# Layer 0 of a two-layer attention kernel rewritten: scores laid out keys by queries, both softmax sums taken by pattern matmuls, weight pairs premultiplied

## The chip, the cores and the metric

The kernel runs on one core of one Trainium2 chip. The metric is the device time of one execution in microseconds (us); for the kernel before it is 9794.67 us, the median of three runs between 9791.2 and 9801.31. The profile is of one further execution of the same program. Its engines are PE (TensorE, the matrix engine, with its weight loads listed apart as PEld), DVE (VectorE), ACT (ScalarE), POOL (GpSimd) and SP (SyncE, which issues transfers).

## The reference

The input `x` has 8 batches of 1024 tokens (64 by 16) of 128 channels, all in fp32. Two layers follow one another.

```python
# layer 0: H = 8 heads, tokens (l, f) and (m, g), 64 by 16
scores = einsum('bhlfc,bhmgc->bhlfmg', q, k) / sqrt(c)
a = softmax(scores, axis=4)          # over m
a = softmax(a, axis=5)               # of the result, over g
z = einsum('bhlfmg,bhmgc->bhlfc', a, v)
z1 = layer_norm(z @ wo.T + bo + x)
x = layer_norm(relu(z1 @ w1.T + b1) @ w2.T + b2 + z1)
# layer 1: additive attention, then a recurrence over the 1024 tokens
Wi = norm(t) @ W.T
scores = einsum('d,bijd->bij', v, tanh(Wi[:, None] + Wi[:, :, None]))
t = t + softmax(scores) @ norm(t)
wx = batch_norm(norm(t) @ W2.T)
y_t = sigmoid(wx_t + y_{t-1} @ V.T);  t = t + y
```

So layer 0 takes two softmaxes in a row over the same 1024 keys of each query: the first sums over the 64 values of m for each g, the second over the 16 values of g for each m. Layer 1 takes a tanh for every pair of tokens; the scores are symmetric, so about half of them are computed.

## The kernel before, in words

All matmuls are fp32. A matmul of the program shows in the trace as two MATMUL instructions over the same columns; a transpose shows as one.

`layer0(b)` is a generator for one batch; each `yield` ends a piece. It transposes `x` into `xT` (channels by tokens). For each of 8 heads it projects `qT`, `kT` (L174, L175) and `vh` (L181, L184). Then for each tile of 128 queries: scores `sc` in PSUM, queries on the partitions and the 1024 keys along the free side (L194); maximum over m (L199), subtraction (L200), exponential on ACT (L203), sum over m (L205), reciprocal (L206), product (L207), second exponential (L209), sum over g (L211), reciprocal (L212) and a product on POOL (L213). Eight transposes on PE and two copies on DVE turn the result into `aT` (L155, L156). For every second query tile, `pz` = `vh` times `aT` (L222), and `po` projects that with `wo` (L228) and is added to `xa` (L233). A query tile is one piece; with 64 tiles, the two layer norms and the feed-forward part, a batch has 71 pieces.

`layer1_attention(b)` goes through eight row blocks of 128 tokens, `it`, of width w = 1024, 896, ..., 128 columns. For each row an ACT tanh fills a `th` buffer (L305; five buffers), and matmuls with a 32-column weight pattern add v times that into 32 partitions of `sa` (L308); the row's group c = 0..3 selects which 32. Columns beyond 512 need a second matmul. After each block come the softmax of the block and its product with B (L316 to L340).

The order. The main loop first runs all of `layer0(0)`. Then, for each batch b, it takes three pieces of `layer1_attention(b)` (each piece is four rows, that is four tanhs) and one of `layer0(b+1)`, until both are done. So 71 layer-0 pieces fall beside the first 213 of 258 attention pieces. The tile framework then decides each engine's final order at compile time: it simulates the program, and gives an engine the oldest instruction in program order that is ready and has a buffer. On the chip each engine's order is fixed. The chip's 8 PSUM banks are shared out as `sc` 2, `sa` 2 and a ring `bank` of 4 for all else.

After the last batch comes the recurrence (L385 to L428), and at its end a branch that would redo it step by step if a bound on V did not hold.

Of the kernel before, what the change touches and what calls it, by code (L numbers as in the profile page):

```python
# [17 lines left out]


@with_exitstack  # L20
def kernel(
    ctx: ExitStack,
    tc: tile.TileContext,
    x: bass.AP,
# [23 lines left out]
):  # L48

    nc = tc.nc
    NB, N, C = x.shape
    H = wq.shape[1]
# [13 lines left out]
        t = keep.tile([P, NT, C], F32, tag=f"xa{b}", name=f"xa{b}")  # L70
        xa.append(t)

    NCH = 64
    LCH = N // NCH
    wx = keep.tile([P, LCH, NCH, NB], F32, tag="wx", name="wx")
    wx_stats = keep.tile([P, NB, N // 512, 6], F32, tag="wx_stats", name="wx_stats")

    def load_x(b):
# [56 lines left out]
    def norm(dst, src, mv, rs, j):  # L135
        nc.vector.tensor_scalar(dst, src, mv[:, j, 0:1], rs[:, j : j + 1], ALU.subtract, ALU.mult)
# [11 lines left out]
    def bank(name):  # L148
        return ps_m.tile([P, 512], F32, tag="bank", name=name)
# [119 lines left out]
    def layer1_attention(b):  # L269
        X = xa[b]  # L270

        def normed_and_projected(w, use):

            B = l1.tile([P, NT, C], F32, tag="B", name="B")
            mv, rs = norm_stats(X, NT, "n1")
            for j in range(NT):
                norm(B[:, j, :], X[:, j, :], mv, rs, j)
            for s in range(NT // 4):
                bT = l1.tile([P, 512], F32, tag="bT", name="bT")
                transposed(bT, [B[:, 4 * s + i, :] for i in range(4)])  # L280
                pw = bank("pw")
                nc.tensor.matmul(pw, w, bT, start=True, stop=True)
                use(s, pw)
            return B

        wiT = l1.tile([P, N], F32, tag="wiT", name="wiT")

        def keep_wi(s, pw):
            nc.vector.tensor_copy(wiT[:, s * 512 : (s + 1) * 512], pw)

        B = normed_and_projected(wa_sb, keep_wi)
        yield


        low = l1.tile([P, NT * (NT - 1) // 2, P], F32, tag="low", name="low")
        for it in range(NT):
            i0 = it * P
            w = N - i0
            sa = ps_a.tile([P, N], F32, tag="sa", name="sa")
            for r in range(32):  # L300

                for c in range(4):
                    i = i0 + 32 * c + r
                    th = l1.tile([P, N], F32, tag="th", name="th", bufs=5)
                    nc.scalar.activation(th[:, :w], wiT[:, i0:], AF.Tanh, bias=wiT[:, i : i + 1])  # L305
                    for s0 in range(0, w, 512):
                        s1 = min(s0 + 512, w)
                        nc.tensor.matmul(  # L308
                            sa[32 * c : 32 * c + 32, s0:s1], vpat[:, 31 - r : 63 - r], th[:, s0:s1],
                            start=(r == 0), stop=(r == 31),  # L310
                        )
                yield
            row = it * (it - 1) // 2
            mine = low[:, row : row + it, :]
            R = l1.tile([P, N], F32, tag="R", name="R")
            nc.vector.tensor_copy(R[:, i0:], sa[:, :w])  # L316
            for j0 in range(it + 1, NT, 4):
                js = range(j0, min(j0 + 4, NT))
                pt = bank("plow")
                for k, j in enumerate(js):  # L320
                    nc.tensor.transpose(pt[:, k * P : (k + 1) * P], R[:, j * P : (j + 1) * P], ident)
                for k, j in enumerate(js):
                    nc.vector.tensor_copy(low[:, j * (j - 1) // 2 + it, :], pt[:, k * P : (k + 1) * P])
            if it:
                nc.vector.tensor_copy(R[:, :i0].rearrange("p (t c) -> p t c", c=P), mine)
            mx = l1.tile([P, 1], F32, tag="mx1", name="mx1", bufs=2)
            nc.vector.tensor_reduce(mx, R, AX.X, ALU.max, negate=True)
            den = l1.tile([P, 1], F32, tag="den", name="den", bufs=2)
            nc.scalar.activation(R, R, AF.Exp, bias=mx, accum_out=den)
            nc.vector.reciprocal(den, den)  # L330
            rT = l1.tile([P, NT, P], F32, tag="rT", name="rT")
            for s in range(NT // 4):
                transposed(
                    rT[:, 4 * s : 4 * s + 4, :],
                    [R[:, (4 * s + i) * P : (4 * s + i + 1) * P] for i in range(4)],
                )
            pc = bank("pc")
            for j in range(NT):
                nc.tensor.matmul(pc[:, :C], rT[:, j, :], B[:, j, :], start=(j == 0), stop=(j == NT - 1))
            nc.vector.scalar_tensor_tensor(X[:, it, :], pc[:, :C], den, X[:, it, :], ALU.mult, ALU.add)  # L340

        def keep_wx(s, pw):
            nc.vector.bn_stats(out=wx_stats[:, b, s, :], in_=pw)
            cs = slice(s * 512 // LCH, (s + 1) * 512 // LCH)
            nc.vector.tensor_copy(
                wx[:, :, cs, b].rearrange("p l c -> p c l"), pw.rearrange("p (c l) -> p c l", l=LCH)
            )

        normed_and_projected(wf_sb, keep_wx)
        yield  # L350
# [17 lines left out]
    main.close()  # L368


    rn = ctx.enter_context(tc.tile_pool(name="rn", bufs=1))
    mv = rn.tile([P, 2], F32, tag="mvb", name="mvb")
    nc.vector.bn_aggr(out=mv, in_=wx_stats.rearrange("p b s k -> p (b s k)"))
# [7 lines left out]


    ys = rn.tile([P, NB, N], F32, tag="ys", name="ys")
    for l in range(LCH):
        nc.vector.tensor_scalar(wx[:, l], wx[:, l], sc, off, ALU.mult, ALU.add)  # L385

    def recurrence_by_chunks(ps_w):  # L390
        HC = NCH // 2
        prev = [None, None]
        for k in range(2 * LCH):
            l = k % LCH
            early = k < LCH
            for half in range(2):
# [11 lines left out]

                    nc.vector.memset(y[:, 0:1, :], 0.0)
                if not early:  # L410
                    steps = ys.rearrange("p b (c l) -> p c b l", l=LCH)
                    nc.vector.tensor_copy(steps[:, c0:c1, :, l], y)
                prev[half] = y

    def output(ps_t, pool):
        n = 0
        for g in range(NT // 4):
            for b in range(NB):
                pt = ps_t.tile([P, 4, C], F32, tag="yt", name="yt")
                for i in range(4):  # L420
                    nc.tensor.transpose(pt[:, i, :], ys[:, b, (4 * g + i) * P : (4 * g + i + 1) * P], ident)
                ot = pool.tile([P, 4, C], F32, tag="ot", name="ot")
                nc.vector.tensor_tensor(ot, pt, xa[b][:, 4 * g : 4 * g + 4, :], ALU.add)
                eng = nc.sync if n % 2 else nc.scalar
                eng.dma_start(
                    out=out[b, 4 * g * P : 4 * (g + 1) * P, :].rearrange("(t p) c -> p t c", p=P), in_=ot
                )
                n += 1  # L428

    with tc.tile_pool(name="ps_w", bufs=2, space=PSUM) as ps_w, tc.tile_pool(  # L430
        name="ps_t", bufs=2, space=PSUM
    ) as ps_t, tc.tile_pool(name="ot", bufs=3) as pool:

        pn = ps_t.tile([P, 4, C], F32, tag="yt", name="pn")
        nc.tensor.matmul(pn[:, 0, :], vf_sb, vf_sb, start=True, stop=True)
        rows = rn.tile([P, 1], F32, tag="rows", name="rows")
        nc.vector.tensor_reduce(rows, pn[:, 0, :], AX.X, ALU.add, apply_absolute_value=True)
        nc.tensor.transpose(pn[0:1, 1, :], rows, ident)
        most = rn.tile([1, 1], F32, tag="most", name="most")
        nc.vector.tensor_reduce(most, pn[0:1, 1, :], AX.X, ALU.max)  # L440
        fits = rn.tile([1, 1], mybir.dt.int32, tag="fits", name="fits")
        nc.vector.tensor_scalar(fits, most, 1.05, None, ALU.is_le)

        recurrence_by_chunks(ps_w)
        output(ps_t, pool)
        fit = nc.values_load(fits[0:1, 0:1], min_val=0, max_val=1,
                             skip_runtime_bounds_check_because="the result of a comparison")


    with tc.If(fit == 0):  # L450
        with tc.tile_pool(name="ps_w1", bufs=2, space=PSUM) as ps_w, tc.tile_pool(
            name="ps_t1", bufs=2, space=PSUM
        ) as ps_t, tc.tile_pool(name="ot1", bufs=3) as pool:
            for t in range(N):
                c, l = t // LCH, t % LCH
                acc = ps_w.tile([P, NB], F32, tag="acc1", name="acc1")
                nc.tensor.matmul(acc, ident, wx[:, l, c, :], start=True, stop=t == 0)
                if t:
                    nc.tensor.matmul(acc, vf_sb, ys[:, :, t - 1], start=False, stop=True)
                nc.scalar.activation(ys[:, :, t], acc, AF.Sigmoid)  # L460
            output(ps_t, pool)


# [55 lines left out]
```

## Time and profile before

| what | value |
|---|---|
| median of three runs | 9794.67 us |
| the profiled execution's own time | 9793.98 us |
| its span, first to last instruction | 9792.2 us |
| PE busy / weight loads busy | 8684.9 us / 3812.2 us |
| ACT busy | 6697.6 us |
| DVE busy | 5528.9 us |
| POOL busy | 1124.6 us |
| first tanh of batch 0, of batch 7 | at 848 us, at 8984 us |
| one batch between (first tanh to first tanh) | 1160 to 1165 us, seven times |

Busy time is the union of an engine's instructions. Matmuls are pipelined and their ends are modelled, so a PE that is busy is not PE at its peak. A wait is idle time of an engine in front of an instruction, named by what ended it last.

### The profile page before, as it was taken

Reading aid. Unit: us, or ns where it says so; the run is one execution under the profiler, and the core shown is the slowest. Engines: PE = TensorE matmul, PEld = TensorE weight load, DVE = VectorE, ACT = ScalarE, POOL = GpSimd, SP = SyncE. Lnnn points to the kernel's source line nnn. Section 1 sums busy time; section 2 is a strip of 40 time slices with the busy share of each in tenths; the row PEclk is TensorE's granted clock in tenths of the full one; section 3 lists DMA queues with packets and bytes.
Section 4 is the critical chain, followed back from the end, with each engine's and each line's share of the span. In section 5 each row is a group of like instructions: output and inputs, shape, how many; then the busy total and the mean of one; then the engine's idle time right before and its main releaser. Section 6 shows DMA issues by size and latency. Waiting matters only on the chain.

```text
span 9792.2 us, 105080 instructions
## 1 busy us (share of the span) xinstructions
PE 8684.9 (89%) x40543; PEld 3812.2 (39%) x40543; DVE 5528.9 (56%) x7379; ACT 6697.6 (68%) x9410; POOL 1124.6 (11%) x551
## 2 busy tenths in 40 slices
PE   6667999889998999989998899988999899998998
PEld 3333344433444334343344334443344433434334
DVE  7775557635675456744577455764567545673002
ACT  1114777766776777767777677776777677777996
POOL 1111111101111011100111011110111101110000
PEclk7778999999999999999999999999999999999999
DMA  1000000000000000000000000000000000000000
GB/s 33 0 0 0 1 1 1 1 1 1 1 1 1 1 1 1 1 1 1 1 1 1 1 1 1 1 1 1 1 1 1 1 1 1 1 1 1 1 1 18
DMA packets 20442, 18.91 MB, mean 2 GB/s; under 512 B 1504, under 2 KB 19040, under 8 KB 19936
## 3 DMA queue, kind: packets, MB, share of 16 engines
q1 hardware_dynamic: 14272, 8.59, 0.3%
q8 instruction: 321, 5.26, 0.2%
q10 hardware_dynamic: 5664, 3.55, 0.1%
q14 instruction: 185, 1.52, 0.1%
HBM read 7.94 MB, written 4.19 MB: 1 GB/s over the span
## 4 chain that ended last, share of the span: by engine, by line
PE 66%; DVE 19%; POOL 7%; ACT 5%; issue 2%; POOLq 0%; DMA 0%; ACTq 0%; DVEq 0%
PE sa L308 35%; PE pz L222 9%; PE sc L194 8%; POOL e L213 6%; PE pt L155 6%; ACT th L305 3%; DVE s L205 3%; DVE s L211 3%; DVE mx L199 3%; DVE e L200 2%; PE pp L174 2%; DVE e L207 2%; DVE aT L156 2%; DVE s L212 1%; PE pv L181 1%
## 5 line engine op out<-in xcount | busy, mean ns | idle before, releaser
L305 ACT ACTIVATE th<-wiT 128x1024 f32<-128x1024 f32 (+7 forms) x8192 | 5631.0, 761 | 1752.2 <-PE sa L308 1497.9
L308 PE MATMUL sa<-th,vpat 128*32 128x512 f32 (+3 forms) x24576 | 5049.2, 500 | 156.9 <-ACT th L305 129.5
L308 PEld LDWEIGHTS sa<-th,vpat 128*32 128x32 f32 x24576 | 1430.5, 109 | 3280.5 <-issue 1691.6
L213 POOL TENSOR_TENSOR e<-e,s 128x1024 f32<-128x1024 f32 x512 | 1071.2, 2092 | 7072.5 <-DVE s L212 3982.1
L194 PE MATMUL sc<-kT,qT 128*128 128x512 f32 x2048 | 1168.4, 669 | 233.8 <-DVE e L200 232.2
L205 DVE TENSOR_REDUCE s<-e 128x16 f32<-128x1024 f32 x512 | 970.4, 1895 | 392.3 <-ACT e L203 389.7
L155 PE MATMUL pt<-ident,e 128*128 128x128 f32 x4096 | 615.2, 298 | 516.5 <-POOL e L213 515.0
L156 DVE COPY aT<-pt 128x512 f32<-128x512 f32 x1024 | 662.8, 685 | 711.1 <-PE pt L155 708.1
L222 PE MATMUL pz<-aT,vh 128*128 128x256 f32 x4096 | 1048.4, 399 | 3.7 <-DVE aT L156 3.7
L209 ACT ACTIVATE e<-e 128x1024 f32<-128x1024 f32 x512 | 538.8, 1052 | 691.2 <-DVE e L207 686.0
L199 DVE TENSOR_REDUCE mx<-sc 128x16 f32<-128x1024 f32 x512 | 623.1, 1217 | 592.6 <-PE sc L194 592.6
L222 PEld LDWEIGHTS pz<-aT,vh 128*128 128x128 f32 x4096 | 756.6, 195 | 380.4 <-issue 182.9
L203 ACT ACTIVATE e<-e 128x1024 f32<-128x1024 f32 x512 | 535.3, 1046 | 489.2 <-DVE e L200 486.1
L155 PEld LDWEIGHTS pt<-ident,e 128*128 128x128 f32 x4096 | 492.4, 152 | 881.3 <-POOL e L213 835.3
L211 DVE TENSOR_REDUCE s<-e 128x64 f32<-128x1024 f32 x512 | 620.6, 1212 | 158.9 <-ACT e L209 156.4
L207 DVE TENSOR_TENSOR e<-e,s 128x1024 f32<-128x1024 f32 x512 | 660.2, 1290 | 6.3
L194 PEld LDWEIGHTS sc<-kT,qT 128*128 128x128 f32 x2048 | 344.0, 200 | 782.4 <-issue 635.2
L200 DVE TENSOR_TENSOR e<-sc,mx 128x1024 f32<-128x1024 f32 x512 | 620.5, 1212 | 10.6 <-DVE mx L199 0.5
L316 DVE COPY R<-sa 128x1024 f32<-128x1024 f32 (+3 forms) x64 | 47.0, 734 | 922.8 <-PE sa L308 922.8
L224 DVE COPY zT<-pz 128x256 f32<-128x256 f32 x256 | 107.8, 421 | 813.8 <-PE pz L222 813.0
L212 DVE RECIPROCAL s<-s 128x64 f32<-128x64 f32 x512 | 277.8, 542 | 6.5
L132 POOL TENSOR_TENSOR n_rs<-n_rs,neg_half 128x8 f32<-128x8 f32 x32 | 52.2, 1638 | 1502.8 <-DVE n_rs L131 1502.8
(92 smaller groups left out, 3286.2 us busy)
## 6 DMA issues: line engine op xcount, KB each, us to landing
xa<-in_x_dram SPq DMA_DIRECT2D x8, 512.0 KB, 7.1
out_dram<-ot ACTq DMA_DIRECT2D x8, 256.0 KB, 2.2
out_dram<-ot SPq DMA_DIRECT2D x8, 256.0 KB, 2.3
wk_sb<-in_wk_dram ACTq DMA_DIRECT2D x1, 512.0 KB, 4.7
wq_sb<-in_wq_dram SPq DMA_DIRECT2D x1, 512.0 KB, 6.4
bv_sb<-in_bv_dram ACTq DMA_DIRECT2D x1, 512.0 KB, 8.3
wv_sb<-in_wv_dram SPq DMA_DIRECT2D x1, 512.0 KB, 8.2
wo_sb<-in_wo_dram SPq DMA_DIRECT2D x1, 512.0 KB, 5.2
```

What stands on the lines that cost most here:

```text
L155: nc.tensor.transpose(pt[:, i * P : (i + 1) * P], t, ident)
L156: nc.vector.tensor_copy(dst, pt[:, : len(tiles) * P])
L194: nc.tensor.matmul(sc[:, cols], qT[:, q0 : q0 + P], kT[:, cols], start=True, stop=True)
L199: nc.vector.tensor_reduce(mx, sc.rearrange("p (m g) -> p g m", g=G), AX.X, ALU.max)
L200: nc.vector.tensor_tensor(e3, sc3, mx.unsqueeze(1).to_broadcast([P, M, G]), ALU.subtract)
L205: nc.vector.tensor_reduce(s1, e.rearrange("p (m g) -> p g m", g=G), AX.X, ALU.add)
L207: nc.vector.tensor_tensor(e3, e3, s1.unsqueeze(1).to_broadcast([P, M, G]), ALU.mult)
L211: nc.vector.tensor_reduce(s2, e3, AX.X, ALU.add)
L213: nc.gpsimd.tensor_tensor(e3, e3, s2.unsqueeze(2).to_broadcast([P, M, G]), ALU.mult)
L222: nc.tensor.matmul(pz[:, :QG], vh[:, t, :], aT[:, t, :], start=(t == 0), stop=(t == NT - 1))
L305: nc.scalar.activation(th[:, :w], wiT[:, i0:], AF.Tanh, bias=wiT[:, i : i + 1])
L308: nc.tensor.matmul(sa[32 * c : 32 * c + 32, s0:s1], vpat[:, 31 - r : 63 - r], th[:, s0:s1], start=(r == 0), stop=(r == 31),)
```

## The change

- Weights are combined once at the start: `A` = Wq'Wk and `Wvo` = Wv'Wo for each head. Scores become `xT`' (A `xT`): one projection `u` in place of q and k. The product with V gives the projected output at once, and the product with `wo` is gone.
- Scores lie keys by queries: 128 keys on the partitions, 512 queries along the free side. A unit of work is one head for 512 queries; 16 units make a batch. The exponentials `e` are then already laid out for the product with V, so the transposes and their copies are gone. No maximum is subtracted; a check computes bounds on the scores.
- Sums over m or over g are now across partitions. They are taken by matmuls with 0/1 patterns of 32 columns: `over_m` (s1) and `over_g` (s2). The reciprocals are spread back by matmuls with `back_m` (r1b) and `back_g` (r2b), and DVE multiplies from PSUM. POOL is out of the loop.
- `x` comes in transposed as well, laid out by the host; `xa` is now written only after the heads.
- The pieces are smaller (four, two or four per phase of a unit) and are handed out in proportion to an estimate of the attention's work, `done`, over the whole attention.
- `sa` keeps 2 banks, `sc` keeps 2 (now two key tiles of 512 queries), `zT` has 1 of its own, and the ring `bank` has 3. The tiles `R`, `rT` and `bT` of layer 1 share the five `th` buffers.
- `check_bounds` reads `x` once more, tile by tile, and forms a flag `fits`. After the fast path a branch runs the old computation, `general_path`, if the flag is 0.

The core of the diff; the removed lines are those of `layer0` and of the main loop printed above.

```diff
+    fast_path(tc, a, fits)
+    fit = tc.nc.values_load(fits[0:1, 0:1], min_val=0, max_val=1, ...)
+    with tc.If(fit == 0):
+        general_path(tc, *[a[n] for n in names.split()])
...
+        for i in range(2):
+            nc.vector.tensor_reduce(over_m[:, i, :], ident.rearrange("p (m g) -> p g m", g=G), AX.X, ALU.add)
...
+        for dst, left, right in ((A, wqn, wkn), (Wvo, wvn, wo)):
+            for g in range(H // 4):
+                pp = bank("pp")
+                for i in range(4):
+                    h = 4 * g + i
+                    nc.tensor.matmul(pp[:, i * C : (i + 1) * C], left[:, h, :], right[:, h, :], start=True, stop=True)
+                nc.vector.tensor_copy(dst[:, 4 * g : 4 * g + 4, :], pp.rearrange("p (h c) -> p h c", c=C))
...
+    def check_bounds():
+        for b in range(NB):
+            two = l0.tile([P, 2, N], F32, tag="e", name="two", bufs=2)
+            xb, sq = two[:, 0, :].rearrange("p (t c) -> p t c", c=C), two[:, 1, :]
+            nc.sync.dma_start(out=xb, in_=a["x"][b].rearrange("(t p) c -> p t c", p=P))
+            nc.gpsimd.tensor_tensor(sq3, xb, xb, ALU.mult)
+            nc.vector.tensor_reduce(n2, sq3, AX.X, ALU.add)
...
+    def layer0(b, xT):
+        for hg in range(2):
+            vp = l0.tile([P, NT, H // 2, C], F32, tag="vp", name="vp")
+            for t in range(NT):
+                pv = bank("pv")
+                nc.tensor.matmul(pv3, xT[:, t * P : (t + 1) * P], Wvo[:, 4 * hg : 4 * hg + 4, :], start=True, stop=True)
+                nc.vector.tensor_copy(vp[:, t], pv3)
+                if t % 2:
+                    yield
+            for qh in range(N // QH):
+                yield from heads(xT, vp, zs, hg, qh)
+        yield from after_heads(X, zs)
+
+    def heads(xT, vp, zs, hg, qh):
+        zT = ps_z.tile([P, QH], F32, tag="zT", name="zT")
+        for h in range(4 * hg, 4 * hg + 4):
+            pu = bank("pu")
+            nc.tensor.matmul(pu, A[:, h, :], xT[:, q0 : q0 + QH], start=True, stop=True)
+            nc.vector.tensor_scalar(u, pu, ub[:, h : h + 1], None, ALU.add)
+            e = l0.tile([P, NT, QH], F32, tag="e", name="e", bufs=2)
+            s1 = bank("s1")
+            for tp in range(NT // 2):
+                sc = ps_s.tile([P, 2, QH], F32, tag="sc", name="sc")
+                for i in range(2):
+                    nc.tensor.matmul(sc[:, i, :], xT[:, t * P : (t + 1) * P], u, start=True, stop=True)
+                nc.scalar.activation(e[:, 2 * tp : 2 * tp + 2, :], sc, AF.Exp, scale=SCALE)
+                for i in range(2):
+                    for qc in range(4):
+                        nc.tensor.matmul(
+                            s1[32 * qc : 32 * qc + 32, :P], over_m.rearrange("p i g -> p (i g)"),
+                            e[:, t, qc * P : (qc + 1) * P], start=t == 0, stop=t == NT - 1,
+                        )
+                yield
+            nc.vector.reciprocal(r1, s1[:, :P])
+            r1b = bank("r1b")
+            for qc in range(4):
+                nc.tensor.matmul(r1b[:, qc * P : (qc + 1) * P], back_m[:, qc].rearrange("p m g -> p (m g)"), r1, ...)
+            s2 = bank("s2")
+            for tq in range(2):
+                nc.vector.tensor_tensor(e4, e4, r1b.unsqueeze(1).to_broadcast([P, 4, QH]), ALU.mult)
+                nc.scalar.activation(e4, e4, AF.Exp)
+                for i in range(4):
+                    for q in range(2):
+                        r0 = 32 * (2 * q + tq)
+                        nc.tensor.matmul(
+                            s2[r0 : r0 + 32, :256], over_g[:, i].rearrange("p i m -> p (i m)"),
+                            e[:, 4 * tq + i, q * 256 : (q + 1) * 256], start=i == 0, stop=i == 3,
+                        )
+                yield
+            nc.vector.reciprocal(r2, s2[:, :256])
+            for t in range(NT):
+                r2b = bank("r2b")
+                for q in range(2):
+                    nc.tensor.matmul(r2b[:, q * 256 : (q + 1) * 256], back_g[:, t, q].rearrange("p m g -> p (m g)"), r2, ...)
+                nc.vector.tensor_tensor(e[:, t, :], e[:, t, :], r2b, ALU.mult)
+                nc.tensor.matmul(zT, vp[:, t, h % 4, :], e[:, t, :], ...)
+                if t % 2:
+                    yield
...
+            bT = l1.tile([P, 512], F32, tag="th", name="bT", bufs=5)
...
+        widths = [N - it * P + 220 for it in range(NT)]
...
+                done += widths[it] / (32 * sum(widths))
+                yield done
...
+    for _ in layer0(0, xT0):
+        pieces += 1
+    for b in range(NB):
+        nxt = layer0(b + 1, load_xT(b + 1, nc.sync)) if b + 1 < NB else iter(())
+        emitted = 0
+        for done in layer1_attention(b):
+            while emitted < done * pieces:
+                next(nxt, None)
+                emitted += 1
+            if b == 0 and not checked and done > 0.1:
+                check_bounds()
```

`after_heads` does what the end of the old `layer0` did, in two halves of 512 tokens (transposes of `zs` back to tokens, layer norm, feed-forward, layer norm), six pieces in all. A batch has 178 pieces.

## The prediction

> **What bounds the kernel now.** I first cut the span into stages with the timeline of ACT: the first tanh of batch 0 starts at 848 us, of batch 7 at 8984 us, and the batches between take 1160 to 1165 us each. So the span is 848 (layer 0 alone) + 7 x 1162 (attention of one batch beside layer 0 of the next) + 808 (attention alone, recurrence, output). Then I asked for busy times by stage.
>
> ```profile
> 16.00:768.00 752.00, 461.53 (x1512) 282.66 (x1510) 575.03 (x667) 132.12 (x125) 139.17 (x62) 0.74 0.02 5
> 3174.00:4337.00 1163.00, 1058.16 (x5027) 454.20 (x5026) 687.70 (x912) 834.76 (x1168) 139.02 (x68) 0.97 0.00 1
> 8984.00:9117.00 133.00, 131.82 (x507) 45.92 (x508) 0.00 (x0) 133.00 (x129) 0.00 (x0) 0.98 0.00 1
> ```
>
> Columns: stretch, us, then PE, PEld, DVE, ACT, POOL busy, the granted clock, DMA. Alone, layer 0 keeps DVE busy for 575 of 752 us and PE for 462 at a clock of 0.74: a chain led by DVE. Alone, attention is bound by ACT (133 of 133). Together, ACT has 835 us of work in 1163, yet PE shows 1058. What holds ACT, in the waits of one batch:
>
> ```profile
> ACT th L305 <- PE sa L308: 211.1, 124, 10.9
> ACT e L209 <- DVE e L207: 64.1, 35, 6.1
> ACT th L305 <- DVE wiT L289: 52.6, 2, 27.4
> ...
> PE pt L155 <- POOL e L213: 49.5, 39, 5.0
> PE sa L308 <- ACT th L305: 18.1, 28, 3.0
> ```
>
> The largest wait is for a `th` buffer, which PE frees by `sa`. So here PE sets the pace, but part of its time is elastic. The timeline shows why:
>
> ```profile
> 3001.27 1.34 PE L308 MATMUL sa<-th,vpat 128*32 128x384 f32 x4 [0.80 <-ACT th L305]
> ...
> 3002.54 1.98 PE L194 MATMUL sc<-kT,qT 128*128 128x512 f32 x4
> ...
> 3006.18 1.09 PE L155 MATMUL pt<-ident,e 128*128 128x128 f32 x8 [0.88 <-POOL e L213]
> ...
> 3007.21 0.85 PE L308 MATMUL sa<-th,vpat 128*32 128x384 f32 x8
> 3007.99 3.72 PE L222 MATMUL pz<-aT,vh 128*128 128x256 f32 x16
> ```
>
> Four rows' `sa` matmuls (x8) took 0.85 us when all were ready, because the four 32-column groups run together; two rows that came one by one took 1.34. In the batch from 3174, `sa` has 624.78 us of PE.
>
> ```profile
> 3174.00:4337.00 1163.00, 624.78 (x3072) 171.09 (x3072) 5.84 (x8) 0.97 0.00 1
> 3174.00:4337.00 1163.00, 140.21 (x256) 40.64 (x256) 0.97 0.00 1
> 3174.00:4337.00 1163.00, 128.97 (x512) 91.59 (x512) 0.97 0.00 1
> ```
>
> (`sa`, `sc`, `pz`.) The `pz` run gives the streaming rate: about 0.215 us for 256 columns, 0.84 ns a column. All `sa` in full groups of four would be 32 x 2 x 4608 columns x 0.84 ns = 248 us, and 299 with 0.2 us for the end of each of 256 groups. So about 325 of the 625 us is the price of single rows.
>
> **DVE, ACT, POOL.** For each query tile the old chain costs DVE, by its rows, 1.217 + 1.212 + 1.895 + 0.239 + 1.290 + 1.212 + 0.542 + 2 x 0.685 = 8.98 us, 575 us a batch. A new unit stands for four tiles: `u` 0.75 (as L175), two products of 2048 elements (twice 1.2 each) 4.8, eight of 512 (as L423, 0.69) 5.5, reciprocals of 128 and 256 elements 0.95 and 1.75 (the line through 239 ns at 16 and 542 at 64), 0.69 for V: 14.4 us, 230 a batch. DVE falls from 688 to about 343 us a batch, and POOL's 139 go; both were off the limit beside attention, so this shortens only layer 0 alone. ACT keeps its elements: 4 x 1.05 + 2 x 1.9 (0.83 ns an element) = 8.0 us a unit against 4 x 2.1, or 829 us a batch.
>
> **PE.** Removed in a batch, by the same stage's rows: transposes 77, `pp` 30, `pv` 16, `po` 22, together 145 us. `sc` (140) and `pz` (129) keep their columns. Added: `u` and V, 64 passes at 0.475 (as `pp`), 30; r1b, 128 at 0.125, 16; r2b, 512 passes of 256 columns, priced as `pz`, 129. The pattern sums have only `sa` for a row. s1 is 128 groups of eight passes of 128 columns, four side by side: 0.21 us a group by rate (27 us) to all passes in line (110); I take 45, near the rate, as its four matmuls are adjacent and read the same tile. s2 is 128 pairs, two side by side: 55 us by rate, 110 in line; I take 65. Added 285, net +140 us a batch (bounds +112 to +250). Were all else equal, PE would show 1058 + 140 = 1198 us.
>
> **What `sa` will cost then** decides. More layer-0 work in smaller steps cuts `sa` into shorter runs (dearer); a fuller PE lets the five `th` buffers fill, and four rows are always emitted together (cheaper). Bounds: 299 and 625; the row that shows a loaded PE is the x8 one, and the x4 one shows the other, so I take the middle, 470. PE work is 1198 - 155 = 1043. Its idle time, 105 us now, loses the waits for POOL but gains those of s1 for the exponential and of the product with V for DVE; nothing excludes either, I take 97. One batch: 1140 us, 22 less than now.
>
> **Layer 0 alone.** PE work of a unit is 28.5 us by rate (456 a batch) and 34.6 by the stage's rows. The unit's own chain is some 42 us (scores and exponentials 4 x 3.3, sums and reciprocals 8, second softmax 7, eight steps of r2b, product and V 14), and two `e` buffers allow two at a time. I take 33 x 16 = 528. Loads as now 16, weight products and patterns 12, and from the last head to the first tanh 54 (now 794 to 848): 610, against 848. Ends: 538 by rate, 754 with one unit at a time.
>
> **Small things.** `check_bounds` takes an `e` buffer eight times for a 512 KB load (7.1 us to landing), a square on POOL (2.1) and a reduction (1.2): 83 us with one buffer less beside batch 0; +20, between 0 and 83. `R`, `rT`, `bT` in the `th` ring: 8, between 0 and 64 (one tanh a block). Transposed loads and the branch: as now, 0; they are hidden by 1100 us of attention, and the span ends as before. A ring of three banks instead of four: between 0 and once more the 105 us that PE idles in a batch now; I take 0 and keep the other end for the range.
>
> Sum: 610 + 7 x 1140 + 808 + 28 = 9426 us of span; the profiled execution's time lies 1.8 above its span and 0.7 below the median. I say **9430 us**, 4% faster, its own range 9010 to 9780 (a batch of 1080 to 1190).
>
> **Two rules weighed.** The trace has PE busy 91% of a batch against 454 us (39%) of weight loads. The Trainium skill ("Trainium Kernel Development and Optimization", Performance Expectations) calls matmul busy time a bad measure of the distance to the peak and weight-load time a good one. By that rule PE has room, ACT would bind at about 900 us a batch, and the sum would be 7750; by busy time alone it would be 10,560. The trace sides with neither: `sa` is elastic, `pz` is not. "TensorEngine Tiling (Array Packing)", Key Properties, says that changing the tiling mode drains the engine, which speaks against s1 and s2; here `pz` starts 0.78 us after the eight `sa`, whose columns alone need 0.64, so a change costs at most about 0.14 us.
>
> **Rivals.** (1) Slower: `sa` stays cut into single rows because some 25 layer-0 steps a unit now lie between them. Place: PE, every combined batch; price 155 us a batch over mine, 1302, in all 10,560. It decides from `sa` = 522 us on (a batch of 1192). For: from 3276 to 3290 us, in the widest block, `sa` alternates with `pz` one row at a time. Against: DVE no longer makes layer 0 late. (2) PE fills its groups: `sa` near 299, ACT at 829 binds, with 30 us between batches and some 50 of stalls a batch 910, in all 7820. For: 211 us of ACT's waits are for PE. Against: the first matmuls of a chain still wait in order. (3) The flag comes out 0 and the old path runs after the new one: near 19,000 us. The weights' scale of 0.02 makes the squared bound some 13,000 against 230,400, so hardly.
>
> **How the numbers follow.** About 0.2% is what a measurement can tell from no change. My case (a batch of 1010 to 1192) has 0.50; rival 2, below 1010, 0.10: faster 0.60. Within 0.2%, 0.03. Rival 1 has 0.37, a third of it above 1251 a batch; rival 3 under 0.01 of that. The range leaves out a tenth at each end: 1008 to 1251 a batch, 8500 to 10,200 us.
>
> **What would show it.** First tanh near 610 us and a clock near 0.95 before it; batches of 1140; `sa` near 470 us of a batch, s1 and s2 near 110, POOL out, DVE near 343; ACT still waiting for `sa`. I am wrong if `sa` does not shrink, if s1 or s2 run in line, or if ACT's exponentials make PE wait in order.

## The result and the profile after

The changed kernel takes 10148.56 us (median of four runs, 10141.56 to 10154.59), the kernel before 9792.99 us beside it: a ratio of 1.0361, 95% interval 1.0343 to 1.0379. It is 3.6% slower; I had said 4% faster. The profiled execution took 10141.56 us, its span is 10139.8. The flag came out 1, so the old path did not run.

By the same cuts as before (first tanh of each batch, in the timeline of ACT):

| stage | before | after | predicted |
|---|---|---|---|
| layer 0 alone, to the first tanh | 848 | 801 | 610 |
| seven batches, first tanh to first tanh | 8136 (1160 to 1165 each) | 8501 (1231 for the first, then 1212 each) | 8000 (1140 each, 20 for the bounds) |
| the rest, from the first tanh of batch 7 | 808 | 838 | 808 |
| span | 9792 | 10140 | 9426 with 8 for the shared ring |

So the loss is in the combined batches (+365) and in the last one (+30), and the gain in front of them is 47 instead of 238. The page of the changed kernel; its second row gives the granted clock of PE in 40 equal slices of the span, in tenths of full speed:

```profile
PE 9294.9 (92%) x49698; PEld 3801.6 (37%) x49698; DVE 2539.1 (25%) x3715; ACT 6683.0 (66%) x9154; POOL 76.4 (1%) x64
...
PEclk9999999999999999999999999999999999999999
...
L799 ACT ACTIVATE th<-wiT 128x1024 f32<-128x1024 f32 (+7 forms) x8192 | 5650.4, 763 | 1946.8 <-PE sa L802 1565.1
L802 PE MATMUL sa<-th,vpat 128*32 128x512 f32 (+3 forms) x24576 | 4719.5, 495 | 12.0 <-ACT th L799 6.3
```

DVE has lost more than half of its work, POOL nearly all, and the clock is 0.9 or more in every slice. Yet PE is busier than before, and it waited only 6.3 us for a tanh in the whole span while ACT waited 1565 us for PE to free a buffer. PE sets the pace more than it did. Busy times by stage (stretch, us, then PE, PEld, DVE, ACT, POOL, the granted clock, DMA): layer 0 alone, one combined batch, attention alone.

```profile
24.00:740.00 716.00, 513.99 (x2735) 261.44 (x2735) 223.16 (x220) 126.60 (x96) 0.00 (x0) 0.96 0.00 1
3243.00:4455.00 1212.00, 1133.46 (x6166) 454.47 (x6165) 310.60 (x448) 833.75 (x1136) 7.26 (x6) 0.98 0.00 1
9302.00:10040.00 738.00, 712.42 (x3268) 260.77 (x3268) 40.74 (x94) 693.34 (x1040) 0.00 (x0) 0.98 0.00 1
```

The same for the line of `sa` alone (us, PE, PEld, clock):

```profile
3243.00:4455.00 1212.00, 575.68 (x3072) 153.89 (x3072) 0.98 0.00 1
```

`sa` cost 576 us of the batch, where I had 470 and the kernel before 625. The timeline of PE in the widest row block of a batch shows what keeps it there (start, us, instruction, count, and in brackets the idle time before and what ended it):

```profile
3299.79 0.28 PE L679 MATMUL r1b<-r,back_m 128*128 128x128 f32 x1
3300.00 1.90 PE L802 MATMUL sa<-th,vpat 128*32 128x512 f32 x4
3301.83 0.49 PE L679 MATMUL r1b<-r,back_m 128*128 128x128 f32 x2
3302.25 1.93 PE L802 MATMUL sa<-th,vpat 128*32 128x512 f32 x12
...
3313.47 0.70 PE L702 MATMUL r2b<-r,back_g 128*128 128x256 f32 x2
3314.09 1.90 PE L802 MATMUL sa<-th,vpat 128*32 128x512 f32 x4
3315.93 0.48 PE L702 MATMUL r2b<-r,back_g 128*128 128x256 f32 x1
```

A row of this block is four passes (x4). One row between two pieces of `r1b` or `r2b` took 1.90 us; three rows together took 1.93. Counted in the trace, the widest block's `sa` comes in 86 runs between other PE work where the kernel before had 52, the narrowest in 34 instead of 3; a whole batch has 463 runs instead of 261. But `sa` as a whole fell, from 625 to 576 us. Many of the new runs stand beside s1 or s2, which use the 32-column groups too (1312 of the 3072 `sa` instructions of a batch). Counted only between matmuls over all 128 columns, there are 310 runs instead of 261, and 101 instead of 94 of one row or less. So rows are still taken singly, about as often as before.

A second loss shows where one row block ends and the next begins. The groups of ACT's tanhs by shape, in the nine microseconds before the exponential of `R`, first before (9112 to 9121 us), then after (9430 to 9439), both in the last batch, where no layer 0 runs beside:

```profile
L305 ACT ACTIVATE th<-wiT 128x1024 f32<-128x1024 f32 x5 | 5.3, 1132 | 0.0
L305 ACT ACTIVATE th<-wiT 128x896 f32<-128x896 f32 x3 | 2.9, 1027 | 0.0
```

```profile
L799 ACT ACTIVATE th<-wiT 128x1024 f32<-128x1024 f32 x6 | 6.3, 1133 | 0.0
```

And the timeline of ACT after:

```profile
9424.81 10.48 ACT L799 ACTIVATE th<-wiT 128x1024 f32<-128x1024 f32 x10
9439.94 1.15 ACT L824 ACTIVATE R<-R,mx 128x1024 f32<-128x1024 f32 x1 [4.65 <-DVE mx L822]
9440.99 0.19 ACT L824 ACTIVATION_READ_ACCUMULATOR R<-R,mx 128x1 f32 x1
9441.08 3.83 ACT L799 ACTIVATE th<-wiT 128x896 f32<-128x896 f32 x4
9446.30 1.04 ACT L799 ACTIVATE th<-wiT 128x896 f32<-128x896 f32 x1 [1.39 <-PE pc L834]
```

Before, ACT ran three rows of the next block (896 columns) while DVE formed the maximum of this one. After, it ran none, waited 4.65 us, and later once more for `pc`, which reads `rT`. Such gaps add up to 33 us in the last batch. In a combined batch, measured from the last tanh of a block to the first of the next, the seven gaps are 55 us after and 5 before, while the eight blocks themselves sum to the same (1125 and 1128 us).

### The profile page after: what moved, and what is told of

Its sections match the earlier page's. It is cut to its first block, busy times and chain, and to the rows that moved or that the text cites. A ratio compares the mean times of both kernels' runs of the same rounds, so it can differ in the third digit from the quotient of the medians.

```text
span 10139.8 us, 116917 instructions
## 1 busy us (share of the span) xinstructions
PE 9294.9 (92%) x49698; PEld 3801.6 (37%) x49698; DVE 2539.1 (25%) x3715; ACT 6683.0 (66%) x9154; POOL 76.4 (1%) x64
## 4 chain that ended last, share of the span: by engine, by line
PE 82%; DVE 9%; ACT 7%; issue 1%; POOL 1%; DMA 0%; DVEq 0%; ACTq 0%; POOLq 0%
PE sa L802 36%; PE r2b L702 10%; PE sc L665 10%; PE zT L707 10%; PE s L692 4%; PE s L670 3%; ACT e L688 3%; DVE e L686 3%; ACT e L666 2%; DVE r L698 2%; PE pc L834 2%; ACT th L799 2%; PE r1b L679 1%; PE pv L640 1%; PE pu L656 1%
## 5 line engine op out<-in xcount | busy, mean ns | idle before, releaser
L702 PE MATMUL r2b<-r,back_g 128*128 128x256 f32 x4096 | 1126.3, 401 | 106.9 <-DVE r L698 106.9
L706 DVE TENSOR_TENSOR e<-e,r2b 128x512 f32<-128x512 f32 x1024 | 703.6, 688 | 2068.3 <-PE r2b L702 1916.7
L666 ACT ACTIVATE e<-sc 128x1024 f32<-128x1024 f32 x512 | 521.5, 1018 | 953.5 <-PE sc L665 952.2
L665 PE MATMUL sc<-u,xT 128*128 128x512 f32 x2048 | 1081.5, 631 | 21.8 <-DVE u L658 20.9
L707 PE MATMUL zT<-e,vp 128*128 128x512 f32 x2048 | 1034.5, 619 | 7.1 <-DVE e L706 7.1
L702 PEld LDWEIGHTS r2b<-r,back_g 128*128 128x128 f32 x4096 | 706.6, 189 | 648.4 <-issue 341.6
L692 PE MATMUL s<-e,over_g 128*32 128x256 f32 x4096 | 532.3, 428 | 280.1 <-ACT e L688 280.1
L686 DVE TENSOR_TENSOR e<-e,r1b 128x2048 f32<-128x2048 f32 x256 | 574.2, 2284 | 363.0 <-PE r1b L679 238.2
L688 ACT ACTIVATE e<-e 128x2048 f32<-128x2048 f32 x256 | 487.3, 1904 | 236.3 <-DVE e L686 235.7
L670 PE MATMUL s<-e,over_m 128*32 128x128 f32 x8192 | 430.2, 279 | 121.8 <-ACT e L666 115.8
```

Source lines behind the costliest of these rows:

```text
L665: nc.tensor.matmul(sc[:, i, :], xT[:, t * P : (t + 1) * P], u, start=True, stop=True)
L666: nc.scalar.activation(e[:, 2 * tp : 2 * tp + 2, :], sc, AF.Exp, scale=SCALE)
L670: nc.tensor.matmul(s1[32 * qc : 32 * qc + 32, :P], over_m.rearrange("p i g -> p (i g)"), e[:, t, qc * P : (qc + 1) * P], start=t == 0, sto ...
L686: nc.vector.tensor_tensor(e4, e4, r1b.unsqueeze(1).to_broadcast([P, 4, QH]), ALU.mult)
L688: nc.scalar.activation(e4, e4, AF.Exp)
L692: nc.tensor.matmul(s2[r0 : r0 + 32, :256], over_g[:, i].rearrange("p i m -> p (i m)"), e[:, 4 * tq + i, q * 256 : (q + 1) * 256], start=i ...
```

## The experiments

Four questions: the shared ring (Theory 1), the bank ring that pieces of layer 0 pass through (Theory 3), rows of `sa` one by one (Theory 5), and how much one more `th` buffer gives (Theory 7). The texts on record number them so; other numbers in them are rivals. All these kernels compute the same outputs. All but the last two ran once; where a kernel was repeated, its runs lay within about 0.1% (9791 to 9801 us for the kernel before). With each edit the framework orders the whole program anew, so an edit can move more than it names. "Batch" is first tanh to first tanh in the middle of the run. The kernel before took 9796.33 us beside the first four runs, 9795.57 beside the next four, and 9794.16 beside the last four.

**The shared ring, put alone on the kernel before.**

```diff
-                bT = l1.tile([P, 512], F32, tag="bT", name="bT")
+                bT = l1.tile([P, 512], F32, tag="th", name="bT", bufs=5)
...
-            R = l1.tile([P, N], F32, tag="R", name="R")
+            R = l1.tile([P, N], F32, tag="th", name="R", bufs=5)
...
-            rT = l1.tile([P, NT, P], F32, tag="rT", name="rT")
+            rT = l1.tile([P, NT, P], F32, tag="th", name="rT", bufs=5)
```

> The kernel before with one edit: R, rT and bT of layer 1 take their buffers from the five of th, as in the changed kernel. Theory 1 (the shared ring holds up the first tanh of the next row block): gaps of some 5 us between row blocks in batch 7 and 7 to 13 us in the other batches, so about 7 x 49 + 30 = 370 us more, near 10,165 us. Theory 2 (the gaps come from layer-0 matmuls standing in the way at a block's end): no more than 30 us more, near 9800 to 9820 us.

It took 10263.01 us, 467 more than the kernel before. The gaps between blocks became 114 us a batch and 33 in the last one, a batch 1220 to 1227 us, and the rest from the last batch on 840 instead of 808; I had expected 370 more in all. ACT at the same change of blocks, by timeline:

```profile
9549.83 4.26 ACT L305 ACTIVATE th<-wiT 128x1024 f32<-128x1024 f32 x4
9558.73 1.15 ACT L329 ACTIVATE R<-R,mx 128x1024 f32<-128x1024 f32 x1 [4.64 <-DVE mx L327]
```

The 4.64 us are the changed kernel's 4.65. The edit alone makes the gap; nothing else of the change is needed for it.

**The ring undone in the changed kernel.** Own buffers for `R` and `rT` need 8 KB a partition. So V' is first made for two heads at a time instead of four (`a_vp2`, the control, which by itself moves little), and then `R` and `rT` get their own tiles (`a_vp2_own`).

```diff
-        for hg in range(2):
-            vp = l0.tile([P, NT, H // 2, C], F32, tag="vp", name="vp")
+        for hg in range(4):
+            vp = l0.tile([P, NT, 2, C], F32, tag="vp", name="vp")
```

> The changed kernel with the heads taken in four groups of two instead of two groups of four, which frees 8 KB a partition and is a control for the next kernels. Both theories: within 60 us of the changed kernel's 10,149 us, as PE streams the same columns and DVE gets 16 more small copies and two more additions a batch.

```diff
-            R = l1.tile([P, N], F32, tag="th", name="R", bufs=5)
+            R = l1.tile([P, N], F32, tag="R", name="R")
...
-            rT = l1.tile([P, NT, P], F32, tag="th", name="rT", bufs=5)
+            rT = l1.tile([P, NT, P], F32, tag="rT", name="rT")
```

> The control with buffers of their own for R and rT (bT stays in the ring). Theory 1: the gaps between row blocks close, from 7 to 13 us to 0 or 1, so about 370 us less than the control, near 9780 us; the first tanh stays at about 801 us. Theory 2: the gaps stay and the time is that of the control within 40 us.

The control took 10098.77 us with 56 us of gaps in a batch of 1205; with own tiles it was 9915.10, gaps 7, a batch 1184 and the rest 810 (`bT` stays in the ring). The 184 us, half of the 370 expected, are what the shared ring costs here: 20 to 25 in each of seven batches and 30 in the last. Of the 49 us of gaps in a combined batch, the blocks took most back by growing from 1115 to 1147 us, probably because PE had used the gaps for other work: in the control it was busy with instructions other than `sa` for 32 of the 56 us. `sa` did not move (all engines, then `sa` alone, of one batch of `a_vp2_own`):

```profile
3181.00:4366.00 1185.00, 1117.31 (x6201) 456.54 (x6200) 315.54 (x470) 832.78 (x1137) 7.26 (x6) 0.99 0.00 1
```

```profile
3181.00:4366.00 1185.00, 573.37 (x3072) 153.51 (x3072) 0.99 0.00 1
```

So the ring is a true loss, but without it the changed kernel is still 119 us over the kernel before.

**Layer 0 alone: the first tiles of a unit in a bank of their own.**

```diff
-    ps_m = main.enter_context(tc.tile_pool(name="ps_m", bufs=3, space=PSUM))
+    ps_m = main.enter_context(tc.tile_pool(name="ps_m", bufs=2, space=PSUM))
+    ps_e = main.enter_context(tc.tile_pool(name="ps_e", bufs=1, space=PSUM))
...
-            pu = bank("pu")
+            pu = ps_e.tile([P, 512], F32, tag="early", name="pu")
...
-            s1 = bank("s1")
+            s1 = ps_e.tile([P, 512], F32, tag="early", name="s1")
```

> The changed kernel with one of the three ring banks set apart for pu and s1. Theory 3 (units run one after another because the ring's banks are given out in program order, so that the next unit's pu and s1 stand behind the last r2b): units overlap, a unit of layer 0 alone falls from 43.7 us to about 30, the first tanh from 801 to about 600 us, and the whole by 200 us or more, to 9950 us or below. Theory 4 (the chain of a unit, or PE's order, keeps units apart whatever the banks): first tanh at 800, time within 50 us of 10,149.

It took 10054.78 us, 94 less than the changed kernel; the first tanh came at 763 us instead of 801, far from 600. The timeline of PE in the changed kernel shows one unit of layer 0 alone:

```profile
112.00 1.02 PE L656 MATMUL pu<-xT,A 128*128 128x512 f32 x2
113.87 1.98 PE L665 MATMUL sc<-u,xT 128*128 128x512 f32 x4 [0.84 <-DVE u L658]
116.97 0.65 PE L670 MATMUL s<-e,over_m 128*32 128x128 f32 x16 [1.11 <-ACT e L666]
...
129.71 1.16 PE L679 MATMUL r1b<-r,back_m 128*128 128x128 f32 x8 [1.08 <-DVE r L676]
135.25 4.49 PE L692 MATMUL s<-e,over_g 128*32 128x256 f32 x32 [4.38 <-ACT e L688]
141.60 1.99 PE L702 MATMUL r2b<-r,back_g 128*128 128x256 f32 x8 [1.86 <-DVE r L698]
```

Every step waits for the one before it, and no other unit's work fills the waits: from `u` to `u` a unit takes 44.4 us (the text above has 43.7). With its own bank the next unit gets only its `u` and its first scores out early, and a unit still takes 41.5 us. Theory 3 had said about 30, Theory 4 no change. The bank ring is a small part; why two units do not interleave further was not separated.

**Both together.** `a_own_bank` has both edits on the changed kernel.

> The changed kernel with groups of two heads, own buffers for R and rT, and a bank of its own for pu and s1. Against the same without the bank (9915 us): theory 3 took 38 us off the first tanh and 7 us off a batch, so here about 90 us less, near 9825 us. If PE alone sets the pace beside attention: first tanh near 765 us, batches as without the bank, 1184, near 9870 us.

9883.34 us, a first tanh at 761, a batch of 1185 to 1188: near the end with PE alone setting the pace (9870), not the other (9825). With the two suspected side effects out, the rewrite is still 0.9% above the kernel before. What remains is the batch. One batch, all engines (columns as above), then `sa` alone (PE, PEld, DVE, clock):

```profile
3137.00:4325.00 1188.00, 1149.93 (x6200) 455.43 (x6198) 313.96 (x469) 833.62 (x1136) 7.27 (x6) 1.00 0.00 1
```

```profile
3137.00:4325.00 1188.00, 601.47 (x3072) 160.88 (x3072) 6.05 (x8) 1.00 0.00 1
```

Against `a_vp2_own` the bank raised `sa` from 573 to 601 us, yet the batch only from 1184 to 1187. So a difference in the busy time of `sa` is not the same difference in the batch.

**Rows in fours.** The matmuls of four rows are held until the fourth tanh is there, so that all run side by side. That needs a `th` buffer more (six) so that ACT can go on. First on the kernel before, then on `a_vp2_own`, then with the bank. `r1` and `r2` have one buffer instead of two in the changed ones, to make room.

```diff
-                    th = l1.tile([P, N], F32, tag="th", name="th", bufs=5)
+                    th = l1.tile([P, N], F32, tag="th", name="th", bufs=6)
+                    ths.append(th)
+                first = None
+                for c in (3, 0, 1, 2):
...
+                        if first is None:
+                            first = mm
+                        else:
+                            tc.add_manual_dep(mm.ins, first.ins.name, ...)
```

> The kernel before; the sa matmuls of four rows are put in PE's order behind the one of the fourth row, so that PE takes four rows at a time, and the th ring has 6 buffers. Theory 5 (single rows of sa are what makes PE set the pace beside layer 0): sa falls from 625 us of a batch to about 330, a batch from 1162 to 900 to 1050 us, the whole to 8000 to 9000 us. Theory 6 (PE's busy time there only stretches to fill what other engines' chains leave): sa falls, but a batch stays above 1120 us and the whole within 300 us of 9796 us; waits for the fourth tanh may even add to it.

> The changed kernel with groups of two heads, own R and rT, the four rows' sa matmuls behind the fourth row's, 6 th buffers. Theory 5: sa falls from some 575 us a batch towards 330 and, since PE has 1130 us of work in a batch of 1184, a batch falls to 900 to 1050 us, the whole to 8000 to 9000 us. Theory 6: the batch stays above 1120 us, the whole above 9500 us.

> The same with a bank of its own for pu and s1. Theory 5 with theory 3: PE now has room, so overlapping units may use it: 50 to 200 us less than without the bank. Theory 6: as without the bank within 60 us.

| kernel | time | first tanh | batch | `sa` in it | rest |
|---|---|---|---|---|---|
| before, fours, six buffers | 9754.67 | 850 | 1124 to 1137 | 403 | 989 |
| own tiles, fours, six | 9450.63 | 810 | 1089 to 1096 | 374 | 977 |
| the same and the bank | 9192.14 | 763 | 1056 to 1065 | 366 | 984 |

On the changed kernel the batch came out between the ends of Theory 5 (1050 at most) and of Theory 6 (above 1120), and the bank then took off 258 us, more than the 200 that either text allowed. On the kernel before Theory 6 held: `sa` shrank as much, from 625 to 403, but the batch only by 35 us and the whole by 41, where Theory 5 had 8000 to 9000 us in all. One batch of it:

```profile
3110.00:4237.00 1127.00, 855.90 (x5024) 401.81 (x5024) 686.31 (x913) 837.45 (x1168) 140.23 (x68) 0.88 0.00 1
```

and what PE waited for there:

```profile
PE sa L312 <- ACT th L306: 154.9, 120, 4.9
PE pt L155 <- POOL e L213: 68.7, 35, 3.8
```

PE is no longer full: it waits for tanhs and for the chain over POOL, and its clock is 0.88. All three also lose 167 to 184 us in the last batch (against 810 in `a_vp2_own`, 811 in `a_own_bank` and, below, 806 in `b_six`), where attention has PE for itself and holding a row back only delays it.

**The sixth buffer alone.** Since these kernels have one buffer more, it has to be told from the fours. On the kernel before it is one number (`bufs=5` to `bufs=6` in L304); in `a_six` it is that, with the own tiles, the bank and the single `r1`, `r2`, rows one by one.

> The kernel before with six th buffers in place of five and nothing else: the control for the fours on it. Theory 5 (PE sets the pace because it takes rows of sa singly): one buffer more changes little, 9650 to 9800 us, batches within 25 us of 1162. Theory 7 (what the fours gained came from the sixth buffer): the same gain in a batch as with the fours, 1131 us.

> The changed kernel with groups of two heads, own R and rT, own bank for pu and s1, six th buffers, rows of sa taken as they come: the control for the fours on it (9192 us). Theory 5: near 9883 us as with five buffers, not below 9750; sa near 575 us a batch. Theory 7: near 9200 us.

The kernel before with a sixth buffer took 9493.17 us, 301 less, with a batch of 1120. One batch of it, all engines and `sa` alone:

```profile
3091.00:4211.00 1120.00, 1014.53 (x5034) 449.24 (x5032) 687.41 (x915) 832.80 (x1168) 135.54 (x68) 0.98 0.00 1
```

```profile
3091.00:4211.00 1120.00, 587.09 (x3072) 166.54 (x3072) 0.98 0.00 1
```

`a_six` took 9476.14, 407 less than `a_own_bank`, with a batch of 1128. Theory 5 had denied both (not below 9650 and 9750). Theory 7 holds on the kernel before, where the batch is even shorter than with the fours. On the changed kernel it holds in part only: it had 9200, and 284 us are left between `a_six` and the same kernel with fours (9192.14). With six buffers, the ring's tiles and the bank set apart and rows one by one, the two kernels are level (9476 and 9493, one run each). One batch of `a_six`, all engines and `sa` alone:

```profile
3030.00:4158.00 1128.00, 1094.50 (x6197) 447.46 (x6196) 313.46 (x467) 827.99 (x1136) 7.30 (x6) 0.99 0.00 1
```

```profile
3030.00:4158.00 1128.00, 546.48 (x3072) 149.73 (x3072) 0.99 0.00 1
```

PE is now busy for 97% of the batch. So on the kernel before the sixth buffer explains all that the fours seemed to give (with the last batch's loss taken out, the fours would be at 9755 - 184 = 9571 by estimate, above 9493; fours only beside layer 0 were not run on it), and on the changed kernel PE at 1094 us is the limit that is left for the fours to lower.

**Fours only beside layer 0.** Rows are grouped in batches 0 to 6 and run singly in batch 7; `a_fours` is otherwise `a_bank_grp6`. `a_pairs` groups two rows instead of four.

```diff
+                size = 4 if b < NB - 1 else 1
+                for c0 in range(0, 4, size):
```

> As the last of the runs with fours (9192 us), with the fours only in batches 0 to 6, where layer 0 runs beside; batch 7 takes rows as they come. In batch 7 the fours cost 978 - 805 = 173 us, as six buffers make ACT wait for PE there. So 9192 - 173 = 9020 us, ratio to the kernel before 0.92; batches stay at 1060 us.

> The same with rows in twos in place of fours in batches 0 to 6. If ACT's waits for a whole group weigh more than PE's time for sa: batches below 1060 us, in all below 9000 us. If PE's time weighs more: sa between 391 and 575 us a batch, batches near 1120 us, in all near 9430 us.

`a_fours`: 9022.36 us (9019.73 to 9025.50), a ratio to the kernel before of 0.9211, interval 0.9196 to 0.9227. `a_pairs`: 9067.36 (9062.42 to 9069.75), 0.9257, interval 0.9241 to 0.9272. One batch of `a_fours`, all engines and `sa` alone:

```profile
2906.00:3969.00 1063.00, 930.48 (x6196) 403.82 (x6195) 312.88 (x468) 830.22 (x1136) 7.26 (x6) 0.96 0.00 1
```

```profile
2906.00:3969.00 1063.00, 367.81 (x3072) 97.87 (x3072) 0.96 0.00 1
```

The timeline of PE there, in the widest block:

```profile
3002.52 1.94 PE L809 MATMUL sa<-th,vpat 128*32 128x512 f32 x16
3006.12 1.92 PE L693 MATMUL s<-e,over_g 128*32 128x256 f32 x16 [1.66 <-ACT e L689]
3007.98 1.98 PE L666 MATMUL sc<-u,xT 128*128 128x512 f32 x4
```

Four rows, sixteen passes, take 1.94 us, where above one row alone took 1.90. Against `a_six` the only edit is the grouping: `sa` falls by 179 us a batch, the batch by 65, and the time by 454, about 7 x 65. It is the fastest version on record, and came out at the 9020 us expected. `a_pairs` met neither end of its text: `sa` is 450 us there, a batch 1068 to 1070. Two rows together bring 409 of the 454 us.

## Why the prediction was wrong

**Where it failed: "What `sa` will cost then".** I took 470, the middle between full groups and single rows. It measured 576, above the 522 at which my first rival was to decide; the batch measured 1212, above its 1192. Rows stay cut, as that rival says: 101 runs of one row or less stand between matmuls over all columns, 94 before. That more and smaller steps make `sa` dearer, which the rival and I both took, did not come out as a whole: its runs rose from 261 to 463 a batch while `sa` fell by 49 us, many of them standing beside s1 and s2. What I had wrong is how far it would fall. That single rows are a price that can be lowered is shown by `a_six` against `a_fours`, with six buffers; with five it was not tried. One more buffer, with single `r1` and `r2`, took `sa` from 601 to 546 and a batch from 1187 to 1128. My argument that "a fuller PE lets the five `th` buffers fill" brought no fuller groups: ACT waited for a buffer that `sa` frees for 221 us of the batch, 211 before, and still PE took rows singly, since its order is fixed and layer 0's steps stand between them.

In PE's own account the batch lies 72 us over my 1140: 105.7 more for `sa`, 15.2 less for other work (558 against 573) and 18.5 less of idle time (79 against 97). By causes, the shared ring has about 21 of the 72 (`a_vp2_own` against `a_vp2`) and V' in four heads about 7 (`a_vp2` against the changed kernel). The 44 left I put down to `sa` by subtraction; no run shows them, and the bank's 28 us of `sa` for 3 us of batch says that the two need not go together. Seven times 44 is 308 us; the other misses are 191 in layer 0 alone, 176 for the ring (184 less 8) and 49 for V'. None of them decides the sign by itself: less the 308 the kernel would be near 9841 by estimate, and with the ring undone (and V' in four groups) it measured 9915, both above the kernel before. Batches of 1140, with all the rest as measured, would have given 801 + 8000 + 838 = 9639, faster than before.

**"`R`, `rT`, `bT` in the `th` ring: 8, between 0 and 64".** It measured 184 us in the changed kernel and 467 on the kernel before, outside the bounds. I counted one tanh a block. But a block change takes two of five buffers for `R` and `rT` until the softmax and `pc` are done, and ACT runs no row of the next block until `R` has its exponential. About 5 us go at each of seven changes in the last batch and 8 at each in a combined one. In which order the framework hands out these buffers was read from the timeline, not tested by itself.

**Layer 0 alone, 610.** It measured 801. The clock (0.96 for 0.95) and the unit's chain (44.4 us for 42) were about right, but I took 33 us a unit between 34.6 and the rate, where the end I had written down for one unit at a time, 754, was nearest. Two `e` buffers did not make two units run together here. The bank ring accounts for some 40 of the 191 us, the rest stays open.

**What held.** The added work on PE, in the batch from 3243 us: r2b 143 (129), s1 and s2 together 121 (110), r1b 21 (16), `u` and V 36 (30). DVE 311 (343), ACT 834 (829), POOL 7. The first batch, which holds `check_bounds`, was 19 us longer than the others (20 expected); that difference is 4 in the kernel before, which has no such check, and 5 to 23 in the other changed kernels, so the check's own cost is not shown. Less the 33 us of gaps, the rest from the last batch on is as before (805 against 808). The bank ring of three was costed at nothing in a batch: moving two tiles out of it left a batch within 7 us (1212 and 1205), and without the shared ring it was 1184 and 1187.

**The two rules.** PE was busy 94% of a batch against 37% in weight loads (454 of 1212). By "Trainium Kernel Development and Optimization", Performance Expectations, weight-load time is the good measure of the distance to the peak and matmul time a bad one; by that there is room. `a_fours` shows some, 65 us a batch less than `a_six`. But the weight loads fell with the grouping too (150 to 98 us for `sa`), and the batch ended 230 us above ACT's work. By busy time alone, the kernel before with fours (856 of 1127) should have gained 202 us a batch; it gained 35, and the sixth buffer alone gives 43. Neither figure says what a batch will cost; the waits did. "TensorEngine Tiling (Array Packing)", Key Properties, has a change of tiling mode drain the engine. In the runs s1 and s2 together came to 121 us, 10% over my price and 39 over the 82 by rate; what part of the 39 is such a change was not separated.

**The rivals.** Rival 1 was right in its side and in that rows stay cut, too dear in its price (1302 against 1212), since `sa` went to 576 and not to 625. Its 155 us over my 1140 make 1295, not 1302, and 10,511 us in all. Rival 2, PE filling its groups by itself, did not occur; forced to, as in `a_fours`, it gives 1063 a batch rather than 910: ACT still waits 191 us there for a `th` buffer, and 26 us for scores.

## What to carry to other kernels

When an engine's cost depends on what lies between its instructions, a rewrite of the other work changes that cost: price it by the steps that will lie between and by their kind (beside s1 and s2 a pass was cheap), and force the grouping rather than hope for it. A small ring of buffers that paces the limiting pair of engines is a resource like the engines; before lending it to another tile, ask how long that tile holds it, and try one buffer more first. Where a work-saving rewrite brings nothing, look for the coupling it ran into: this one came out 8% under the kernel before once rows were grouped and the ring had six buffers, while the kernel before got 3% from the sixth buffer and nothing further from the grouping in all batches.

## What the runs showed of the hardware that I had not expected

- Four rows on four 32-column groups cost as much as one: 1.94 us for sixteen passes in a run, 1.90 for the four passes of a single row between two matmuls over all columns. Between steps of s2, which uses the groups too, a single pass is cheap: a stretch of 32 passes of s2 with 6 of `sa` among them, from 3306.71 to 3311.47 us of the changed kernel, took 4.76 us, where 32 of s2 in runs of sixteen take 3.84 (twice 1.92 in `a_fours`); 0.15 us for each `sa` pass.
- In the combined batches the mean granted clock went roughly with PE's busy time: 0.88 in the kernel before with fours (856 of 1127 us), 0.96 in `a_fours` (930 of 1063), 0.98 with the sixth buffer alone (1015 of 1120), 1.00 in `a_own_bank` (1150 of 1188). Busy time alone does not set it: layer 0 alone had 0.96 at 514 of 716 us. What the lower clock cost was not measured.
- One `th` buffer more, six for five, moved the kernel before by 301 us and the changed one (with its own tiles and bank, and single `r1` and `r2`) by 407, each about as much as the rewrite itself had cost (356).
